# Two chained attention blocks on one core: the f, g, h projections as one block product of 20 instead of 22, with f spilled to DRAM and PSUM in fixed banks

## The chip, the core and the metric

The kernel runs on one core of a Trainium2 chip, in float32 throughout. The metric is device time in microseconds (us) of one launch: the median of three runs before the change is 2583.78 us (2582.63 to 2584.57).

## The reference, cut to what matters

`x` is (8, 512, 64, 64). Two layers follow each other, each added to its input:

```python
def layer0(x):                                  # attention with pooled keys and values
    f = conv1x1(x, Wf, bf)                      # 64 channels x 4096 pixels
    g = maxpool2x2(conv1x1(x, Wg, bg))          # 64 channels x 1024
    v = maxpool2x2(conv1x1(x, Wh, bh))          # 256 channels x 1024
    beta = softmax(einsum('bcn,bcm->bnm', f, g), axis=-1)
    o = einsum('bcm,bnm->bcn', v, beta)         # 256 channels x 4096
    return gamma * conv1x1(o, Wv, bv) + x

def layer1(x):                                  # linear attention
    Q, K, V = wq x + bq, wk x + bk, wv x + bv
    Qf, Kf = delu(Q).T, delu(K)                 # delu(z) = 10*relu(z) + exp(10*min(z, 0))
    KV = einsum('bmn,bcn->bmc', Kf, V)
    norm = 1 / einsum('bnd,bd->bn', Qf, sum(Kf) + 1e-10)
    return x + gamma * einsum('bnd,bdc,bn->bcn', Qf, KV, norm)
```

## The kernel before

The 4096 pixels of an image are cut into 8 chunks of 512, so there are 64 chunks in all (`TOTAL`). One call of `step(s)` works on three things at once: the softmax attention and the layer-1 features of chunk `s` (stage B), the f, g and h projections of chunk `a = s + 9` (stage A; `LEAD` is 9), and the layer-1 end of two chunks of the image before (stage C, on odd steps `finish`). So there are 9 leading steps with stage A alone, 55 middle steps (`s` = 0 to 54) in which A and B run together, and the last image's tail. From `s` = 8 on the odd middle steps carry stage C's product as well: 23 of the 55.

**The order is written by hand.** Each piece of work is entered with a number, `at(t, fn)`; a step sorts its pieces by that number and issues them in this order, and every engine runs its own instructions in that order. The numbers are only an order.

**Stage A** (`a_fg`, `a_h`): f and g are one 128-row product over four input blocks, four matmuls of 512 columns (L272). h is a 2x2x2 block product after Winograd's scheme: 7 products of two 256-column matmuls each (L316), from four sums of x that GpSimd forms (L305 to L308, 128x512 each). In units of one 128x128x256 product, f and g cost 8 and h costs 14, that is 22. VectorE takes h out of PSUM (L326 to L340), pools g and h with reductions (L249), and ScalarE copies f twice into SBUF (L290), where nine such tiles are kept until stage B is nine steps on.

**Stage B**: `weigh` makes the scores of the next chunk (L410, products `s`) and their exponentials (L414, ScalarE, tile `E`). VectorE adds the eight blocks up (L448, L450, L453, tile `r`), a product with ones gives the totals (L467, `tot`), VectorE inverts them (L477, `rq`), two DMAs through DRAM spread the row over the partitions (L482, L484, `rb`), and `keep_inverses` (L497) copies it into a PSUM bank, from which `normalize_block` (L511) multiplies E. `look` (L501, L502) records two checks on ScalarE. `attend` is again seven products (L535, `M1` to `M7`, four 256-column matmuls each) with VectorE sums around them (L517 to L526 for the operands `T1` to `T4`, L544 to L568 for the results). `project` (L598, `N1` to `N7`) makes layer 0's output; ScalarE evicts parts of it (L608), GpSimd and VectorE add them to x (L611, L614, L619). `features` (L645, `pk`) gives layer 1's K and Q.

**Stage C**: `gather` (L739, `pg`) adds K times x transposed into `G`; `normalize` (L861, `pd`) makes the divisors; `finish` (L898, `pa`) has eight products, each copied out by ScalarE (L901) and added to the output by a GpSimd DMA (L904). The transposes of x and K go through DMA (L682, L700) with splitting and joining copies on ScalarE (L694, L707) and GpSimd (L686, `kT`).

All PSUM tiles come from one pool of eight banks in rotation (`bank`, tag "m", `bufs=8`): a product waits until whoever read the product eight places before it is done.

Of the kernel before, what the change touches and what calls it, by code (L numbers as in the profile page):

```python
# [8 lines left out]
F32 = mybir.dt.float32  # L37
U16 = mybir.dt.uint16
# [13 lines left out]
def tile_two_attention_blocks(  # L52
# [40 lines left out]
    w_fg = const.tile([P, KT, 2 * D], F32, name="w_fg")  # L93
    nc.scalar.dma_start(out=w_fg[:, :, 0:D], in_=WfT.rearrange("(k p) o -> p k o", p=P))
    nc.scalar.dma_start(out=w_fg[:, :, D : 2 * D], in_=WgT.rearrange("(k p) o -> p k o", p=P))
    w_h = const.tile([P, KT, CV], F32, name="w_h")
    nc.scalar.dma_start(out=w_h, in_=WhT.rearrange("(k p) o -> p k o", p=P))
    b_fg = const.tile([P, 1], F32, name="b_fg")
    nc.scalar.dma_start(out=b_fg[0:D], in_=bf.rearrange("(p o) -> p o", o=1))
    nc.scalar.dma_start(out=b_fg[D : 2 * D], in_=bg.rearrange("(p o) -> p o", o=1))  # L100
    b_h = const.tile([P, VT], F32, name="b_h")
    nc.scalar.dma_start(out=b_h, in_=bh.rearrange("(k p) -> p k", p=P))
# [24 lines left out]
    def winograd_weights(name, a11, a12, a21, a22, shape):  # L127

        t = const.tile([P, 4] + shape, F32, name=name)
        s1, s2, s3, s4 = (t[:, i] for i in range(4))  # L130

        def form():
            nc.vector.tensor_tensor(s1, a21, a22, ALU.add)
            nc.vector.tensor_tensor(s2, s1, a11, ALU.subtract)
            nc.vector.tensor_tensor(s3, a11, a21, ALU.subtract)
            nc.vector.tensor_tensor(s4, a12, s2, ALU.subtract)

        return {1: a11, 2: a12, 3: s4, 4: a22, 5: s1, 6: s2, 7: s3}, form


    w_h7, form_w_h7 = winograd_weights(
        "w_h7",
        *(w_h[:, bass.ts(j, KT // 2), bass.ts(i, P)] for i in range(2) for j in range(2)),
        [KT // 2, P],
    )
    form_w_h7()
# [21 lines left out]
    def prepare_late():  # L168
        nc.vector.tensor_scalar(gb_v0, b_v0, g0, None, ALU.mult)
        nc.vector.tensor_scalar(w_v, w_v, g0, None, ALU.mult)  # L170
        form_w_v7()
        nc.vector.tensor_scalar(b10_kq, b_kq, PARAM, None, ALU.mult)
        nc.vector.tensor_scalar(b_v1, b_v1, g1, None, ALU.mult)
# [6 lines left out]
    def run(ctx, general):  # L180
# [4 lines left out]
        fpool = ctx.enter_context(tc.tile_pool(name="fpool", bufs=9))  # L185
# [7 lines left out]
        psum = ctx.enter_context(tc.tile_pool(name="psum", bufs=8, space=bass.MemoryType.PSUM))  # L193

        def bank(name):
            return psum.tile([P, CH], F32, tag="m", name=name)

        def scratch(name):
            return temp.tile([P, CH], F32, tag="t", name=name)

# [7 lines left out]
        def load_a(a):  # L208
# [13 lines left out]
            else:  # L222
                if a == 1:
                    nc.gpsimd.tensor_copy(x_a[a][0:1, 0, 0:1], w_fg[0:1, 0, 2 * D - 1 : 2 * D])
# [15 lines left out]
        fgs, fs, vps = {}, {}, {}  # L240

        th, hs, es, sums, totals, rq, rtots, te, os_, to = ({} for _ in range(10))
# [23 lines left out]
        def a_fg(a, at, t, t_f, t_g):  # L266
            j = a % NCHUNK

            def product():
                fg = fgs[a] = bank(f"fg_{a}")  # L270
                for k in range(KT):
                    nc.tensor.matmul(  # L272
                        fg, w_fg[:, k, :], x_a[a][:, k, :], start=(k == 0), stop=(k == KT - 1)
                    )

            def out_g():

                gp = work1.tile([P, P], F32, tag="gp", name=f"gp_{a}")
                pool(gp[D : 2 * D, :], fgs[a][D : 2 * D, :])
                nc.vector.tensor_scalar(  # L280
                    image_of(a)["g"][half(j % 2), j // 2, :], gp[D : 2 * D, :], b_fg[D : 2 * D],
                    None, ALU.add,
                )

            def out_f():

                fg = fgs[a]
                f = fs[a] = fpool.tile([P, CH], F32, tag="f", name=f"f_{a}")
                for e in range(2):
                    nc.scalar.activation(f[half(e)], fg[0:D], AF.Identity, bias=b_fg[0:D])  # L290

            at(t, product)
            at(t_f, out_f)
            at(t_g, out_g)

        def a_h(a, at, t_sums, t, t_out_3, t_pool):
            hk = KT // 2

            def sums_of_x():
                b11, b12, b21, b22 = (  # L300
                    x_a[a][:, bass.ts(i, hk), bass.ts(j, HN)] for i in range(2) for j in range(2)
                )
                ta, tb = blocks(f"tha_{a}", "T2"), blocks(f"thb_{a}", "T3")
                t1, t2, t3, t4 = (u[:, bass.ts(i, hk), :] for u in (ta, tb) for i in range(2))
                nc.gpsimd.tensor_tensor(t1, b12, b11, ALU.subtract)  # L305
                nc.gpsimd.tensor_tensor(t2, b22, t1, ALU.subtract)
                nc.gpsimd.tensor_tensor(t3, b22, b12, ALU.subtract)
                nc.gpsimd.tensor_tensor(t4, t2, b21, ALU.subtract)  # L308
                th[a] = {1: b11, 2: b21, 3: b22, 4: t4, 5: t1, 6: t2, 7: t3}

            m = {}

            def product(i):
                m[i] = bank(f"H{i}_{a}")[:, 0:HN]
                for k in range(hk):
                    nc.tensor.matmul(  # L316
                        m[i], w_h7[i][:, k, :], th[a][i][:, k, :], start=(k == 0), stop=(k == hk - 1)
                    )

            def copy_1():  # L320
                u = m["m1"] = scratch(f"h1_{a}")
                nc.scalar.copy(u[:, 0:HN], m[1])

            def out_1():
                h = hs[a] = blocks(f"h_{a}", "T4").rearrange("p (v j) n -> p v (j n)", v=VT)
                nc.vector.tensor_tensor(h[:, 0, 0:HN], m["m1"][:, 0:HN], m[2], ALU.add)  # L326

            def out_2():
                h, u, w = hs[a], m["m1"], scratch(f"h2_{a}")
                u2, u3 = u[:, HN:CH], w[:, 0:HN]  # L330
                nc.vector.tensor_tensor(u2, u[:, 0:HN], m[6], ALU.add)
                nc.vector.tensor_tensor(h[:, 0, HN:CH], u2, m[5], ALU.add)
                nc.vector.tensor_tensor(h[:, 0, HN:CH], h[:, 0, HN:CH], m[3], ALU.add)
                m["u2"], m["u3"] = u2, u3

            def out_3():
                h, u2, u3 = hs[a], m["u2"], m["u3"]
                nc.vector.tensor_tensor(u3, u2, m[7], ALU.add)
                nc.vector.tensor_tensor(h[:, 1, HN:CH], u3, m[5], ALU.add)
                nc.vector.tensor_tensor(h[:, 1, 0:HN], u3, m[4], ALU.subtract)  # L340

            def out_pool():
                vp = vps[a] = work1.tile([P, VT, P], F32, tag="vp", name=f"vp_{a}")
                for v in range(VT):
                    pool(vp[:, v, :], hs[a][:, v, :])
# [925 lines left out]
```

## Time and profile before

| | |
|---|---|
| median of 3 runs | 2583.78 us |
| span of the profiled execution | 2581.3 us |
| TensorE matmul busy | 2553.4 us, 11223 records |
| VectorE busy | 1951.9 us (76%) |
| ScalarE busy | 1587.9 us (62%) |
| GpSimd busy | 777.6 us (30%) |
| an even middle step without stage C's product, first M product to first M product | 37.29 us |
| an odd one with it | 40.94 us |

Every float32 matmul shows as two records. A record of 256 columns is listed with a mean of about 380 ns, though the next one starts 216 ns later: records overlap (the page says that matmuls are pipelined and their ends modelled). What a product costs the engine is therefore read from start to start in the timeline, not from the mean. The last two rows of the table come from the timeline of TensorE around the middle of the run.

### The profile page before, as it was taken

To read this page: it belongs to the slowest core of one execution; us is meant where nothing else is said; L and a number is where in the kernel's file an instruction comes from. 1 tells how busy PE (TensorE), PEld (TensorE's weight loads), DVE (VectorE), ACT (ScalarE), POOL (GpSimd) and SP (SyncE) were. 2 spreads that over 40 slices of the span, in tenths; PEclk is the share of its full clock that TensorE was granted. 3 is DMA by queue.
4 is the path that set the end of the run, shared out by engine and by line. 5 is a ranking of instruction groups with operands and counts; after the bars stand their busy time and mean duration, and the time that the engine had idled before them with its cause. 6 is when DMAs were issued, how large, how long until landed. Compare 5 with 4: busy or idle time off the path is not lost.

```text
span 2581.3 us, 32122 instructions
## 1 busy us (share of the span) xinstructions
PE 2553.4 (99%) x11223; PEld 1766.8 (68%) x11223; DVE 1951.9 (76%) x3012; ACT 1587.9 (62%) x2724; POOL 777.6 (30%) x624
## 2 busy tenths in 40 slices
PE   9999999999999999999999999999999999999997
PEld 7667766766767667667667677676676676766664
DVE  5777878777777777777777777777777777788874
ACT  3366567567566566675675665666756756656662
POOL 5422223322323323323333223323234232221112
PEclk9999999999999999999999999999999999999998
DMA  5154456566556666665666565765657655655658
GB/s 174 53 141 115 117 142 166 126 174 152 138 167 148 151 178 130 165 167 131 170 161 153 147 153 141 192 140 147 160 133 188 164 132 146 154 143 145 159 141 273
DMA packets 495068, 392.26 MB, mean 152 GB/s; under 512 B 348409, under 2 KB 363697, under 8 KB 494897
## 3 DMA queue, kind: packets, MB, share of 16 engines
q1 hardware_dynamic: 477648, 330.60, 46.8%
q0 software_dynamic: 15232, 58.72, 12.4%
q8 instruction: 91, 1.49, 0.2%
q10 hardware_dynamic: 2016, 0.79, 0.1%
q14 instruction: 81, 0.66, 0.1%
HBM read 173.41 MB, written 133.39 MB: 119 GB/s over the span
## 4 chain that ended last, share of the span: by engine, by line
PE 95%; DVE 3%; issue 0%; DMA 0%; ACT 0%; POOL 0%; ACTq 0%; DVEq 0%
PE M L535 30%; PE H L316 15%; PE N L598 14%; PE s L410 9%; PE pk L645 9%; PE fg L272 8%; PE pg L739 5%; PE pa L898 4%; DVE E L511 1%; PE tot L467 1%; PE pa L977 1%; PE pkv L834 1%; DVE xb L614 0%; DMA w_h<-in_L_conv_Wh_dram 0%; PE pd L861 0%
## 5 line engine op out<-in xcount | busy, mean ns | idle before, releaser
L611 POOL TENSOR_TENSOR xb<-xb,n 128x512 f32<-128x512 f32 x192 | 245.2, 1277 | 464.3 <-ACT n L608 443.4
L535 PE MATMUL M<-T,S 128*128 128x256 f32 x1536 | 363.4, 387 | 0.0
L535 PEld LDWEIGHTS M<-T,S 128*128 128x128 f32 x1536 | 282.2, 190 | 94.1 <-ACT E L414 28.2
L707 ACT COPY xT<-u 128x1024 uint16<-128x1024 uint16 x252 | 328.3, 1354 | 1.4
L511 DVE TENSOR_TENSOR E<-E,rtot 128x1024 f32<-128x1024 f32 x256 | 304.6, 1212 | 32.4 <-ACT rtot L497 30.1
L608 ACT ACTIVATE n<-N,gb_v 128x256 f32<-128x256 f32 x384 | 160.9, 470 | 254.4 <-PE N L598 251.3
L694 ACT COPY w<-xb 128x1024 uint16<-128x1024 uint16 x252 | 244.8, 1042 | 83.5 <-DVE xb L614 83.5
L414 ACT ACTIVATE E<-s 128x512 f32<-128x512 f32 x512 | 256.2, 617 | 33.1 <-PE s L410 26.9
L686 POOL COPY kT<-uk 128x512 uint16<-128x512 uint16 x56 | 68.0, 1214 | 610.8 <-DMA uk<-wk 610.8
L598 PE MATMUL N<-to,w_v 128*128 128x256 f32 x1024 | 243.0, 380 | 2.6 <-ACT n L608 2.6
L410 PE MATMUL s<-f,g 64*128 64x512 f32 x1024 | 238.6, 602 | 0.3 <-DVE o L544 0.3
L645 PE MATMUL pk<-xb,w_kqk 128*128 128x512 f32 x512 | 230.5, 593 | 2.6 <-DVE xb L619 2.6
L535 PE MATMUL M<-E,vT 128*128 128x256 f32 x1024 | 231.5, 379 | 0.0
L614 DVE TENSOR_TENSOR xb<-xb,N 128x512 f32<-128x512 f32 x256 | 174.7, 684 | 72.8 <-POOL xb L611 70.4
L305 POOL TENSOR_TENSOR tha<-xa 128x512 f32<-128x512 f32 x59 | 78.5, 1331 | 482.1 <-PE M L535 445.0
L598 PEld LDWEIGHTS N<-to,w_v 128*128 128x128 f32 x1024 | 193.3, 190 | 31.4 <-ACT n L608 4.2
L535 PEld LDWEIGHTS M<-E,vT 128*128 128x128 f32 x1024 | 194.5, 190 | 26.9 <-issue 0.5
L272 PE MATMUL fg<-xa,w_fg 128*128 128x512 f32 x472 | 212.3, 592 | 0.0
L448 DVE TENSOR_TENSOR r<-E 128x1024 f32<-128x1024 f32 x64 | 78.4, 1225 | 162.7 <-ACT E L414 162.7
L598 PE MATMUL N<-o,w_v 128*128 128x256 f32 x768 | 188.3, 381 | 1.5 <-ACT n L608 0.9
L598 PEld LDWEIGHTS N<-o,w_v 128*128 128x128 f32 x768 | 144.7, 190 | 56.0 <-issue 34.5
L497 ACT COPY rtot<-rb 128x512 f32<-128x512 f32 x54 | 31.8, 590 | 230.1 <-DMA rb<-rd 230.1
(168 smaller groups left out, 4522.2 us busy)
## 6 DMA issues: line engine op xcount, KB each, us to landing
xb<-in_x_dram SPq DMA_DIRECT2D x64, 1024.0 KB
out_dram<-xb SPq DMA_DIRECT2D x63, 1024.0 KB
xa<-in_x_dram SPq DMA_DIRECT2D x59, 1024.0 KB
out_dram<-y POOLq DMA_DIRECT2D x56, 1024.0 KB, 10.5
rb<-rd SPq DMA_DIRECT2D x54, 256.0 KB
w_v<-in_L_conv_wv_dram SPq DMA_DIRECT2D x8, 1024.0 KB
rn<-rn_row SPq DMA_DIRECT2D x56, 128.0 KB
x_early<-in_x_dram SPq DMA_DIRECT2D x4, 1024.0 KB
```

The costliest lines, as they stand in the source:

```text
L272: nc.tensor.matmul(fg, w_fg[:, k, :], x_a[a][:, k, :], start=(k == 0), stop=(k == KT - 1))
L316: nc.tensor.matmul(m[i], w_h7[i][:, k, :], th[a][i][:, k, :], start=(k == 0), stop=(k == hk - 1))
L410: nc.tensor.matmul(sc[e], g[half(e), i, :], fs[s][half(e), :], start=True, stop=True)
L414: nc.scalar.activation(es[s][:, 2 * i + e, :], sc[e], AF.Exp)
L511: nc.vector.tensor_tensor(b, b, r, ALU.mult)
L535: nc.tensor.matmul(m[i], v7[i][:, k, :], te[s][i][:, k, :], start=(k == 0), stop=(k == hm - 1))
L598: nc.tensor.matmul(a[:, k, :], w_v7[i][:, bass.ts(k, P)], b, start=not more and k == 0, stop=True, skip_group_check=more or k > 0,)
L611: nc.gpsimd.tensor_tensor(of_x(*ij), of_x(*ij), u, ALU.add)
L614: nc.vector.tensor_tensor(of_x(*ij), of_x(*ij), m[i], op)
L645: nc.tensor.matmul(pk, w_kqk[:, i, e * D : (e + 2) * D], x_b[s][:, i, :], start=(i == 0), stop=(i == KT - 1),)
L694: nc.scalar.copy(w, x_b[s][:, k, :].bitcast(U16).rearrange("p (n h) -> p h n", h=2))
L707: nc.scalar.copy(v[:, k], u)
```

## The change

It replaces stage A and moves many pieces of work within a step.

- f, g and h become one product of a 3x4 block matrix of weights and a 4x2 block matrix of x (columns: even and odd pixel rows) with 20 block products, each one 256-column matmul (two records). Its weights (`w_p`, 20 blocks) are formed once, at the start. Its operands are single blocks of x or one of 12 sums, formed by 14 additions of 128x256: all on GpSimd, but for the first four on VectorE in the leading steps.
- The 20 products are added up in five chains, A to E, in four fixed PSUM banks (m4 to m7; D follows E in m7). A chain goes on while its partial sums are read: a reader takes the sum as it stands between two products, and the next product of the chain waits for that reader.
- f goes to DRAM (`store_f`) and comes back two steps ahead of its use (`load_f`).
- PSUM: four banks rotate in the middle steps (m0 to m3); the first four of the scores and of `pa` use m4 to m7.
- `keep_inverses` is gone: `normalize_block` multiplies by the row in SBUF (`rb`).
- ScalarE copies `M3` out at once; VectorE copies one of the eight `pa` products.
- New order: M6, M5, M7, M4 before `pg`, then `pg`, `tot`, `pd` in a row; the four `join_x` copies after the exponentials and the `pa` copies; `look` after the inversion and ahead of stage A's first evictions; `features` behind all 20 products. The scaling of Wv moves from VectorE to GpSimd.

The new order of a middle step on TensorE is: M1, M2, M3, eight `s`, (eight `pa`), M6, M5, M7, M4, `pg`, `tot`, (`pd`), products 1 3 8 14 17 2 4, N1, N2, N4, products 5 7 11, N6, N7, products 6 10, N5, products 13 20 9, N3, products 12 16 19 15 18, `pk`. On VectorE it is, from the exponentials on: three additions to `r`, (the copy of a `pa`), M6's sum, the last addition to `r`, the sums of M5, M7, M4 with the operands of `project`, the inversion, (the second inversion), G's addition, three sums of h, a block of E, a sum of f and g, N2's addition, a sum of h, a block of E, N7's addition, two sums of h, and so on.

```diff
-            psum = ctx.enter_context(tc.tile_pool(name="psum", bufs=8, space=bass.MemoryType.PSUM))
-        def bank(name):
-            return psum.tile([P, CH], F32, tag="m", name=name)
+        ring = {"next": 0, "wide": 0}
+        def bank(name, tag=None):
+            if tag is None:
+                tag = f"m{ring['next'] % ring['size']}"
+                ring["next"] += 1
+            return psum.tile([P, CH], F32, tag=tag, name=name)
+        def wide(name, i):
+            return bank(name, None if i > 3 or ring["size"] == 8 else f"m{4 + i}")
...
+        B_SUMS = (
+            ("v18", "b00", "b31", ALU.subtract), ("v14", "b00", "b01", ALU.add),
+            ("v8", "b01", "b21", ALU.subtract), ("v11", "b00", "v8", ALU.add),
+            ("v20", "b01", "b31", ALU.add), ("v20", "b11", "v20", ALU.subtract),
...
+        CHAIN = {
+            1: "A", 2: "A", 5: "A", 6: "A", 9: "A", 15: "A", 18: "A",
+            3: "B", 4: "B", 7: "B", 10: "B", 12: "B",
+            8: "C", 13: "C", 20: "C",
+            14: "E", 17: "E",
+            11: "D", 16: "D", 19: "D",
+        }
+        HEADS = {1: 4, 3: 5, 8: 6, 14: 7, 11: 7}
...
+            def sums(first, last):
+                for i, (to_, x, y, op) in enumerate(B_SUMS[first:last]):
+                    e = nc.vector if s_early and first == 0 else nc.gpsimd
+                    e.tensor_tensor(operand(to_), operand(x), operand(y), op)
+            def product(p):
+                c = CHAIN[p]
+                if p in HEADS:
+                    tag = HEADS[p] - 4 * (s_early and a % 2)
+                    chains[c] = bank(f"{c}_{a}", f"m{tag}")[:, 0:HN]
+                nc.tensor.matmul(
+                    rows_of(chains[c]), w_p[:, p - 1, :], operand(OPERAND[p]), start=p in HEADS,
+                    stop=True, skip_group_check=True,
+                )
+            def into(to_, c, op):
+                nc.vector.tensor_tensor(to_, to_, chains[c], op)
+            def first_20():
...
+                nc.scalar.activation(h(2, 0), chains["A"], AF.Identity, bias=b_h[:, 1:2])
...
+            at(8.2, sums, 0, 4)
+            at(8.21, sums, 4, 14)
...
+            at(t_first[1], first_20)
...
+            at(24.7, lambda: into(acc["fg"], "A", ALU.add))
+            at(27.41, lambda: into(h(1, 1), "A", ALU.subtract))
...
-        def keep_inverses(s):
-            u, rtots[s] = rtots[s], bank(f"rtot_{s}")
-            nc.scalar.copy(rtots[s], u)
...
+                if i == 3:
+                    os_[s] = work1.tile([P, VT, CH], F32, tag="o", name=f"o_{s}")
+                    nc.scalar.copy(os_[s][:, 0, HN:CH], m[3])
...
+            def copy():
+                nc.vector.tensor_copy(m["y"][:, 0, 0, :], m["pa"])
...
+            if ks[0] == 2 and t < 9.0:
+                at(11.85, copy)
...
-                    1: (0.0, None), 2: (1.7, 3.5), 3: (3.9, None), 6: (14.4, 16.1), 5: (16.2, 20.5),
+                    1: (0.0, None), 2: (1.7, 4.0), 3: (3.45, None), 6: (8.8, 11.9), 5: (10.5, 14.0),
+                    7: (12.2, 14.3), 4: (13.9, 15.9),
...
-                    gather(s - 1, at, *((30.9, 32.6) if late_k else (12.6, 13.5)))
+                    gather(s - 1, at, *((30.9, 32.6) if late_k else (15.8, 17.6) if a <= TOTAL else (12.6, 13.5)))
...
-                    t, t_invert = 16.1 if j % 2 == 1 and c_here else 17.85, 18.0
+                    t, t_invert = 16.0, 17.5
...
-                    at(23.0, keep_inverses, n)
...
+                    at(17.55 if 17.4 < t_invert < 18 and a < TOTAL else 26.0 if t_invert > 22 else 21.5, look, n)
```

The order of GpSimd's work changes with it. Before, in a step: the join of `kT`, two pairs of sums of x (each pair after some of the M products), on odd steps two output DMAs, three additions to x. After: the join of `kT`, on odd steps one output DMA (which waits for four `pa` copies), then all 14 sums of x, the first addition to x, on odd steps the other output DMA, two more additions.

## The prediction

> **What bounds the kernel now.** First the page's shares and slices, then the waits of TensorE, then a step's timeline.
>
> ```profile
> PE 2553.4 (99%) x11223; PEld 1766.8 (68%) x11223; DVE 1951.9 (76%) x3012; ACT 1587.9 (62%) x2724; POOL 777.6 (30%) x624
> ...
> PE 95%; DVE 3%; issue 0%; DMA 0%; ACT 0%; POOL 0%; ACTq 0%; DVEq 0%
> ```
>
> TensorE is busy 99% of the span and makes 95% of the chain that ended last. Its own list of waits is nearly empty:
>
> ```profile
> PE N L598 <- ACT n L608: 3.5, 5, 0.9
> PE pk L645 <- DVE xb L619: 2.6, 3, 1.2
> PE row L1226 <- DVE xb L982: 1.7, 1, 1.7
> ```
>
> A dozen entries, 13.5 us in all. So every product removed is gained in full, and every new wait of TensorE is lost in full. The timeline gives the price of a product:
>
> ```profile
> 1269.11 1.89 PE L535 MATMUL M<-E,S 128*128 128x256 f32 x8
> 1270.93 3.70 PE L410 MATMUL s<-f,g 64*128 64x512 f32 x16
> 1274.56 1.94 PE L739 MATMUL pg<-xT,kT 128*64 128x512 f32 x8
> ...
> 1283.99 3.60 PE L272 MATMUL fg<-xa,w_fg 128*128 128x512 f32 x8
> 1287.43 1.89 PE L598 MATMUL N<-o,w_v 128*128 128x256 f32 x8
> ```
>
> From start to start: `fg` 3.44 us for 8 records of 512 columns. Sixteen M records of 256 columns (1265.66 to 1269.11) take 3.45, so 0.216 each.
>
> **The work of TensorE.** Removed per chunk: 3.44 + 28 records of h x 0.216 = 9.49. Added: 40 x 0.216 = 8.64. The saving is 0.85 per chunk, 54 us over 64. `pg` moves beside `tot`, but the number of passages between whole-array products and narrower ones stays (s and pg in one visit, tot in another; now s in one, pg and tot in the other). The stretches around them run 0.1 to 0.2 over their ideal length, as before: 0. Without a new wait the span would be 2581 - 54 = 2527.
>
> **Wait 1: a ring of four banks.** M6 now follows the scores and takes, four places on, the bank of the fifth score. In the even step that begins at 1265.66 the eight exponentials start at 1272.17 and last 3.94: the fifth is read about 2.9 after the first begins, at 9.0 us into the step; TensorE is there at 8.8. Cost 0.25 (between 0.1 and 0.4). In an odd step with `pa`, M6 takes the bank of the fifth `pa`, which VectorE copies behind its three additions to `r`. In the step at 1224.71 these end at 1237.13, 12.4 into the step; the nearest row for the copy is G's (L746, 690 ns): 13.1, where TensorE is at 12.35. Cost 0.7 (0.5 to 0.9). Queued behind M6 is everything.
>
> **Wait 2: VectorE and GpSimd on one port.** This is the term that decides. VectorE and GpSimd late in the same step:
>
> ```profile
> 1282.51 1.34 POOL L307 TENSOR_TENSOR thb<-xa 128x512 f32<-128x512 f32 x1 [1.04 <-PE M L535]
> 1283.82 1.26 POOL L308 TENSOR_TENSOR thb<-tha,xa 128x512 f32<-128x512 f32 x1
> ...
> 1283.09 0.42 DVE L561 TENSOR_TENSOR o<-u,M 128x256 f32<-128x256 f32 x1
> ...
> 1284.53 0.83 DVE L566 TENSOR_TENSOR to<-o,to 128x256 f32<-128x256 f32 x1
> 1285.29 0.41 DVE L567 TENSOR_TENSOR to<-o 128x256 f32<-128x256 f32 x1
> ```
>
> L561, with one operand in PSUM, keeps its 0.42 under GpSimd's addition. L566, with both operands in SBUF, takes 0.83 and ends 0.28 after GpSimd does; L567, the same shape just after, takes 0.41. At the start it is plainer: three 256-column weight sums took 1.00, 1.48 and 1.48 beside GpSimd's additions, the fourth 0.43. The Trainium skill ("SBUF — State Buffer", section "Who interferes with whom") says why: an instruction of VectorE with two SBUF inputs and one of GpSimd that reads SBUF exclude each other, the loser blocking for the whole of the other's instruction. It speaks against this change twice: GpSimd's sums go from 4 to 14 instructions and move under the additions to `r`, and E's scaling loses its PSUM operand. By the rule's worst case an encounter costs a whole GpSimd instruction. By the row it costs what is left of it: 0.41 of a 1.26-long one for L566, about 0.3 on its mean (734 against 429 ns).
>
> Length of a 128x256 sum on GpSimd: not in the trace; half of 1271 ns (L308) is 0.64 and a line from 0.32 (the 128x64 addition at the start) to 1.27 gives 0.73. I take 0.7, so 14 sums take 9.8, plus what VectorE holds them up. In even steps they start after `kT`, about 8 into the step, and run to 18 or later. Between the exponentials and the inversion VectorE has nine instructions with two SBUF operands (three additions to `r`, the last one, the sum M3 + m1, four operands of `project`). Lost per encounter 0.35, half a sum: about 3. VectorE's slack there is 0.5 before M4's result and 0.6 before `tot`, so the inversion comes 1.9 late (0 if no encounter, 5 by the rule's worst case).
>
> Who waits for the inversion? On ScalarE `look` stands right behind it (two checks, 0.8 by the starts 1281.57, 1281.97), and behind `look` stands `first_20`, which must read chain A before product 2. From `tot`'s start: 0.36 + 0.13 to VectorE, 0.98 inversion, 0.80 `look`, 0.47 `first_20` (L608's row), 0.15 hops: 2.9. TensorE reaches product 2 after tot 0.36 and five products x 0.43: 2.5. Late by 0.4 even without the port, by up to 2.3 with it. For even steps I take 1.3, since some sums fall into gaps (ends 0.4 and 3.5). In odd steps with `pa`, GpSimd's output DMA waits for four `pa` copies (12.5) and takes 1.2, so the sums begin near 13.7, behind the additions to `r`; six encounters remain, 2.1 less 1.1 of slack and 0.3 from `pd`: 0.7 (0 to 1.5).
>
> **Wait 3: product 9.** It needs a sum of h (`at(27.41)`) which stands on VectorE behind N7's addition to x, which waits for GpSimd's addition. From N6's end: 0.2 + 0.84 ScalarE, 1.28 GpSimd, 0.69 + 0.42 VectorE, 0.1: 3.5; TensorE does N7, N5 and four products meanwhile: 3.45. Nearly even; but a scaling of E with two SBUF operands (1.2 us, L511) runs just before, and GpSimd's addition must wait for its end. Up to 1.1; I take 0.8 (0.1 to 1.2).
>
> **What is hidden.** VectorE per step: out go 0.70 + 0.33 + 7 x 0.416 + 2 x 0.68 = 5.3; in come 11 sums x 0.42, 0.48, 0.29, 0.69, 0.43 and half a copy: 6.9. So 30.5 (1951.9 / 64) becomes 32, with some 4 of port waits 36 of 39: covered, barely; if uncovered, each us is a us. ScalarE loses 3.2 (copies of f 2 x 0.68, bias 2 x 0.48, 0.37, `rb` 0.59) and gains about as much: 0. f's DMA, 0.4 MB a step against 6 MB: 0. `xT`'s four copies now follow the exponentials: done 16.2 into an even step, where `pg` stands at 15.9: up to 0.3, inside the ends of wait 1. SP's queue: f's loads wait for the scores to be read, ahead of the inversion's DMA, but that reading is over by then: 0.
>
> **Leading steps.** Before, real products began at 6.75 and 5 us of them were done when w_h's sums came (13.62). Now the first needs ten weight sums and four of x on VectorE beside GpSimd from 9.3 on: about 15 to 18. Loss 8. The nine steps then save 0.85 each if TensorE bounds them and lose up to 1.5 if VectorE does (8.4 of 8.6 us, and seven encounters). I take +6 for all (-5 to +20). The tail keeps its order: 0.
>
> **The sum.** Without stage C's product: -0.85 + 0.25 + 1.3 + 0.8 = +1.5, times 32 = 48. With it: -0.85 + 0.7 + 0.7 + 0.8 = +1.35, times 23 = 31. With +6: +85. The profiled execution, 2581.3, becomes 2666; the median stands 2.5 above it: **2669**.
>
> **Rivals.**
> 1. *Faster: the port hardly costs.* VectorE idles 24%, and 2.5 to 3 us a step before `r`. If the sums of x fall mostly into ScalarE's and TensorE's turns, wait 2 is 0.2 and wait 3 is 0.1, and a step costs -0.85 + 0.45 + 0.3 = -0.1 to, with M6 hidden too, -0.7: 2545 to 2578, say 2560. Against: the slack lies before `r`, the sums after its start. It decides if product 2 waits under 0.4. Chance 0.2.
> 2. *No difference:* saving and waits cancel, 2584. Chance 0.05.
> 3. *VectorE becomes the bound:* encounters cost nearly a whole sum (0.6 x 15 = 9 on 32): 41 a step against 39.1, 55 x 2.2 = +120 and the lead +15: 2719 or above. For: 36 of 39 already. Against: mean loss 0.3 in L566's row. Chance 0.15.
> 4. *The 20 products don't run at 0.216* since their x operand skips every second row: no row shows such a read; 10% would be 0.86 a step, and comes under 3.
>
> My forecast has 0.6, with its own range 2615 to 2715. The range for 8 in 10 is 2578 to 2732. A run tells 0.2% (5 us) from no change: faster 0.2, same 0.05, slower 0.75.
>
> **What would show it.** TensorE's list of waits shows product 2 (on ScalarE) and M6 and product 9 (on VectorE) with about 55 entries each; additions to `r` longer than 1.23 in even steps and not in odd ones; a step of 38.8 and 42.3 from M1 to M1. Wrong, if TensorE's share stays at 98% or above, or if additions to `r` keep 1.23.

## The result and the profile after

| | before | after |
|---|---|---|
| median | 2584.18 us (4 runs) | 2720.89 us (2719.72 to 2724.85, 4 runs) |
| span of the profiled execution | 2581.3 us | 2717.8 us |
| ratio, 95% interval | | 1.0534 [1.0519, 1.0549] |

The change makes the kernel 5.3% slower: 136.7 us on the medians, 136.5 on the spans. The forecast was 2669, so the direction and the range for 8 in 10 (2578 to 2732) held. The loss is 1.6 times the 85 us of the sum, and the time lies 6 us above the range that the forecast had kept for its own account (2615 to 2715), where only the third rival (2719 or above) had put it. First the page of the kernel after, its line of busy times:

```profile
PE 2563.6 (94%) x11471; PEld 1816.8 (67%) x11471; DVE 2199.3 (81%) x3339; ACT 1597.3 (59%) x2847; POOL 1205.9 (44%) x1229
```

TensorE falls from 99% to 94%, while no other engine comes near 100%: no engine has taken its place as the bound, TensorE waits. (The record count is no use for the saved products: a pair shows as two records of 256 columns where f and g had records of 512.) What it waits for, in its own list (waiting instruction, engine and instruction waited for, us in total, times, longest):

```profile
PE A L358 <- DVE h L368: 46.0, 56, 6.1
PE M L637 <- DVE y L1020: 22.5, 23, 1.3
PE A L358 <- ACT h L373: 18.5, 44, 0.8
PE s L516 <- DVE o L649: 8.8, 6, 1.5
PE B L358 <- DVE v L351: 6.0, 1, 6.0
```

Before, the whole list came to 13.5 us. The first three lines are the three waits of the forecast: product 9 (waits for a sum of h), M6 (for the copied `pa`), product 2 (for `first_20` on ScalarE). M6's short waits in even steps are not listed. The fourth and the fifth line were not in the forecast: scores at six places, and the very first product. Times at which M1 begins (from TensorE's timeline) cut the span into pieces, and say how much each group of steps lost:

| piece of the run | before | after | sum of the loss |
|---|---|---|---|
| up to the first product of M | 100.15 | 126.25 | +26.1 |
| step 0 | 38.01 | 42.37 | +4.4 |
| steps 1 to 7, mean | 37.29 | 38.33 | +7.3 |
| first step of an image (6), mean | 37.51 | 44.06 | +39.3 |
| second step of an image (6), mean | 42.82 | 44.68 | +11.1 |
| other even steps (18), mean | 37.29 | 38.34 | +18.9 |
| other odd steps (17), mean | 40.88 | 42.47 | +27.0 |
| steps 55 to 62, and the end | | | +2.5 |

### The profile page after: what moved, and what is told of

Read it like the earlier page. It is cut to its first block, busy times and chain, and to the rows that moved or that the text cites. A ratio compares the mean times of both kernels' runs of the same rounds, so it can differ in the third digit from the quotient of the medians.

```text
span 2717.8 us, 34765 instructions
## 1 busy us (share of the span) xinstructions
PE 2563.6 (94%) x11471; PEld 1816.8 (67%) x11471; DVE 2199.3 (81%) x3339; ACT 1597.3 (59%) x2847; POOL 1205.9 (44%) x1229
## 5 line engine op out<-in xcount | busy, mean ns | idle before, releaser
L716 POOL TENSOR_TENSOR xb<-xb,n 128x512 f32<-128x512 f32 x192 | 282.8, 1473 | 409.4 <-ACT n L713 409.4
L794 POOL COPY kT<-wk 128x512 uint16<-128x512 uint16 x56 | 66.5, 1188 | 873.1 <-DMA wk<-wk 873.1
L637 PEld LDWEIGHTS M<-T,S 128*128 128x128 f32 x1536 | 293.1, 194 | 120.3 <-DVE y L1020 41.5
L802 ACT COPY w<-xb 128x1024 uint16<-128x1024 uint16 x252 | 255.3, 1043 | 175.9 <-DVE xb L719 175.9
L613 DVE TENSOR_TENSOR E<-E,rb 128x1024 f32<-128x1024 f32 x220 | 304.4, 1384 | 64.8 <-DMA rb<-rd 64.1
L351 POOL TENSOR_TENSOR v<-xa,v 128x256 f32<-128x256 f32 x410 | 324.9, 804 | 18.3
L351 POOL TENSOR_TENSOR v<-xa 128x256 f32<-128x256 f32 x345 | 324.5, 1013 | 14.5 <-PE A L358 12.8
L358 PE MATMUL A<-v,w_p 128*128 128x256 f32 x640 | 201.0, 398 | 73.4 <-DVE h L368 46.0
L358 PEld LDWEIGHTS A<-v,w_p 128*128 128x128 f32 x640 | 112.2, 190 | 129.6 <-issue 60.1
L556 DVE TENSOR_TENSOR r<-r,E 128x1024 f32<-128x1024 f32 x128 | 172.3, 1346 | 15.1 <-ACT E L520 2.6
```

The costliest lines, as they stand in the source:

```text
L351: e.tensor_tensor(operand(to_), operand(x), operand(y), op)
L358: nc.tensor.matmul(rows_of(chains[c]), w_p[:, p - 1, :], operand(OPERAND[p]), start=p in HEADS, stop=True, skip_group_check=True,)
L613: nc.vector.tensor_tensor(b, b, r, ALU.mult)
L637: nc.tensor.matmul(m[i], v7[i][:, k, :], te[s][i][:, k, :], start=(k == 0), stop=(k == hm - 1))
L716: nc.gpsimd.tensor_tensor(of_x(*ij), of_x(*ij), u, ALU.add)
L802: nc.scalar.copy(w, x_b[s][:, k, :].bitcast(U16).rearrange("p (n h) -> p h n", h=2))
```

## The experiments

All times are medians; the kernel after is 2720.9, and each ratio is to the kernel before (2583 beside each of them). In a kernel whose edit adds three lines, line numbers behind it are higher by 3.

**Product 9's place in VectorE's order.**

```
-            at(27.41, lambda: into(h(1, 1), "A", ALU.subtract))
+            at(27.05 if a >= LEAD else 27.41, lambda: into(h(1, 1), "A", ALU.subtract))
```

> The sum of h before product 9 is moved ahead of N7's addition to x on VectorE, nothing else. My theory (wait 3 is that place in VectorE's order, behind GpSimd's addition): product 9's wait of 0.7 to 0.85 falls below 0.15, 55 steps x 0.7 = 38: about 2683. Rival A (VectorE is late anyway, by the scaling of E just before): half of the wait stays, about 2700. Rival B (the chain of products only hands the wait on to product 12 or to N5): no change, 2715 to 2722.

Measured: 2679.75 us, ratio 1.0368 [1.0351, 1.0385], 41.1 less. This is the list of TensorE's waits in that kernel:

```profile
PE M L637 <- DVE y L1020: 20.8, 23, 1.2
PE A L358 <- ACT h L373: 15.2, 31, 0.8
...
PE A L358 <- DVE h L368: 6.1, 3, 5.3
```

The line that stood first, 46.0 us in 56 waits, is down to 6.1 us in 3, and most of that is the start. The other two lines stay. So the wait was one place in an order. Nearly nothing was handed on: from `pk` to the next M1 it is now 3.54 us instead of 3.43, since VectorE does the addition to x that `pk` needs behind that sum now.

**`look` behind the first evictions.**

```
-    at(17.55 if 17.4 < t_invert < 18 and a < TOTAL else 26.0 if t_invert > 22 else 21.5, look, n)
+    at(18.45 if 17.4 < t_invert < 18 and a < TOTAL else 26.0 if t_invert > 22 else 21.5, look, n)
```

> The two checks of look move on ScalarE from before first_20 to right behind the four first evictions; nothing else. My theory (inversion late by the port, then 0.80 us of checks before first_20): the wait of product 2 goes, 0.5 in even and 0.3 in odd steps: 22 us, 2697 to 2702. Rival A (product 2 waits for the inversion itself or for the evictions, not the checks): within 5 of 2721. Rival B (the wait goes on to product 5 or to a bank): gain under 8 us.

Measured: 2694.8 us, ratio 1.0432 [1.0414, 1.0449], 26.1 less; even steps 38.34 become 37.77, odd ones 42.47 become 42.05. The list of waits of that kernel, its first lines:

```profile
PE A L358 <- DVE h L368: 48.1, 55, 6.1
PE M L637 <- DVE y L1020: 21.5, 23, 1.3
PE s L516 <- DVE o L649: 8.8, 6, 1.5
```

Product 2's line is gone, and the gain (26) is more than that line had held (18.5): the list counts less than a wait costs.

**GpSimd without its sums of x.**

```
                     e = nc.vector if s_early and first == 0 else nc.gpsimd
-                    e.tensor_tensor(operand(to_), operand(x), operand(y), op)
+                    if s_early:
+                        e.tensor_tensor(operand(to_), operand(x), operand(y), op)
+                    else:
+                        e.memset(operand(to_), 0.25)
```

> Leaves out the 14 sums of x that GpSimd forms per chunk in the steps from the last leading one on (each becomes a fill of the same slot with a constant, so GpSimd reads no SBUF there), and scales the scores by 0.001 within the exponentials so that they stay finite; the order and all other instructions stay. Changed kernel: 2721. My theory (VectorE and GpSimd on one port): additions to r fall from 1.35 to 1.23 us on the mean, product 2's wait of 0.4 to 0.6 in even steps goes below 0.2, even steps 38.3 become 37.6 to 37.8, odd ones 42.5 become 42.1 to 42.3: 2685 to 2700. Rival A (look alone stands before first_20, port or not): product 2 still waits 0.4, 2710 to 2720. Rival B (the banks and the new order cost the time): steps as they were, within 5 of 2721. Product 9's wait of 0.7 should stay by every theory, since its partner is GpSimd's addition to x.

Measured: 2693.5 us, ratio 1.0427 [1.0409, 1.0444], 27.4 less, even steps 37.78, odd ones 42.09. Two stretches of VectorE's and GpSimd's timelines (start, us, instruction) show why. The kernel after, an odd step whose M1 begins at 1388.86, VectorE first and one of GpSimd's sums below it:

```profile
1404.61 0.85 DVE L559 TENSOR_TENSOR r<-r 128x512 f32<-128x512 f32 x1
1405.38 0.94 DVE L658 TENSOR_TENSOR o<-o,m 128x256 f32<-128x256 f32 x1
...
1410.42 0.95 DVE L672 TENSOR_TENSOR to<-o 128x256 f32<-128x256 f32 x1
1411.29 0.94 DVE L673 TENSOR_TENSOR to<-to,o 128x256 f32<-128x256 f32 x1
1412.16 0.94 DVE L583 RECIPROCAL rq<-tot 128x128 f32<-128x128 f32 x1
...
1404.98 1.06 POOL L351 TENSOR_TENSOR v<-xa,v 128x256 f32<-128x256 f32 x1
```

The same step where GpSimd only fills (M1 at 1372.66), VectorE first, GpSimd below it, and last two earlier rows:

```profile
1388.41 0.69 DVE L562 TENSOR_TENSOR r<-r 128x512 f32<-128x512 f32 x1
1389.02 0.42 DVE L661 TENSOR_TENSOR o<-o,m 128x256 f32<-128x256 f32 x1
...
1393.93 0.42 DVE L675 TENSOR_TENSOR to<-o 128x256 f32<-128x256 f32 x1
1394.26 0.42 DVE L676 TENSOR_TENSOR to<-to,o 128x256 f32<-128x256 f32 x1
1395.51 0.96 DVE L586 RECIPROCAL rq<-tot 128x128 f32<-128x128 f32 x1 [0.83 <-PE tot L576]
...
1386.12 4.18 POOL L354 MEMSET v<- 128x256 f32 x14
...
1382.52 2.87 DVE L559 TENSOR_TENSOR r<-r,E 128x1024 f32<-128x1024 f32 x2
...
1383.23 1.14 POOL L797 COPY kT<-wk 128x512 uint16<-128x512 uint16 x1 [16.85 <-DMA wk<-wk]
```

A sum of two SBUF tiles takes 0.94 beside GpSimd's sums and 0.42 without them. The inversion begins 23.3 us into the step with the sums and 22.85 without them, and there it has waited 0.83 for `tot`: VectorE has become early. The fills, which write SBUF and read none, hold nothing up (0.42 for L661 in the middle of them). This is the exclusion of two reads that the forecast took from the Trainium skill ("SBUF — State Buffer", "Who interferes with whom"), which also says that a GpSimd instruction that only writes does not take part; these rows agree. What the theory had wrong is where it bites: the additions to `r` lost little to the sums (1346 ns on the mean, 1310 without them; before 1229). They meet GpSimd's copy `kT`, which is there either way: in the last two rows it runs alone beside them, and they take 2.87 for two, as in the kernel after. It is the sums of 256 columns behind them that double.

**The copy of `pa` between the additions to `r`.**

```
-                at(11.85, copy)
+                at(11.0, copy)
```

> VectorE's copy of the fifth pa moves from behind the three additions to r to before the last of them (time 11.0 in place of 11.85), nothing else. My theory (wait 1: M6 takes that bank, so it waits for the copy's place in VectorE's order): the copy ends 1.4 us earlier, M6's wait of 1.04 in the 23 steps with pa falls below 0.2, 23 x 0.9 = 20: about 2701. Rival A (the last addition to r, now 0.7 later, delays M6's result and the sum for tot): the gain comes back as a wait of tot or product 2, under 8. Rival B (four banks are too few, so M6 then waits for another bank): under 8.

Measured: 2703.8 us, ratio 1.0468 [1.0450, 1.0485], 17.1 less. TensorE's timeline in an odd step of the kernel after (the bracket is the wait just before):

```profile
1316.95 3.60 PE L1011 MATMUL pa<-qq,kv 64*128 64x512 f32 x16
1321.53 5.45 PE L637 MATMUL M<-T,S 128*128 128x256 f32 x24 [0.97 <-DVE y L1020]
```

And with the copy moved:

```profile
1387.46 3.60 PE L1011 MATMUL pa<-qq,kv 64*128 64x512 f32 x16
1390.99 5.45 PE L637 MATMUL M<-T,S 128*128 128x256 f32 x24
```

M6 follows the first `pa` after 3.53 us instead of 4.58. Four banks are enough; what counted was when the one reader got to its bank. Odd steps go from 42.47 to 41.72, so 0.3 of the 1.05 comes back further on in the step.

**The sums of v at the start of an image.** `sums_of_v` makes S1 to S4, the operands of M3, M5, M6 and M7, once an image on GpSimd, four additions of 128x512, at the end of the step before. The change left it alone. The first of two experiments takes it out:

```
-            nc.gpsimd.tensor_tensor(s1, a21, a22, ALU.add)
-            nc.gpsimd.tensor_tensor(s2, s1, a11, ALU.subtract)
...
+            nc.gpsimd.memset(s1, 0.25)
+            nc.gpsimd.memset(s2, 0.25)
...
```

> Leaves out the four sums S1 to S4 of v of each image (they become fills with a constant; GpSimd reads no SBUF there). Theory (at an image's start GpSimd's four 512-wide sums hold VectorE's pooling of h and scaling of E, which now read SBUF twice, and the scores wait): pooling instructions back to 0.69 and 0.42 us, scaling to 1.22, the first steps of images fall from 43 to 44 us to 37.5 to 38.5, six times 5 to 6 us: 2685 to 2692, and the granted clock there stays above 0.95. Rival (the first step of an image is long since M3 now stands 0.45 us earlier and waits for S4 itself, or since the image's first step changed in order): the fills are shorter than the sums, so M3 finds them too, but VectorE's instructions are no shorter; under 10 us gained if the cause is the order.

Measured: 2685.5 us, ratio 1.0391 [1.0374, 1.0409], 35.4 less. First steps of images take 38.49 in place of 44.06; other even ones stay (38.35). The timelines of GpSimd, VectorE and TensorE around such a start in the kernel after, that of the fourth image (M1 at 1099.44):

```profile
1097.36 2.02 POOL L498 TENSOR_TENSOR S<-vT 128x512 f32<-128x512 f32 x1 [4.20 <-ACT vT L479]
...
1098.17 1.76 DVE L413 TENSOR_TENSOR hm<-h 128x512 f32<-128x512 f32 x1
1099.96 1.38 DVE L415 TENSOR_TENSOR vp<-hm 128x256 f32<-128x256 f32 x1
1101.27 2.29 DVE L613 TENSOR_TENSOR E<-E,rb 128x1024 f32<-128x1024 f32 x1
1103.59 2.18 DVE L619 TENSOR_TENSOR T<-E 128x1024 f32<-128x1024 f32 x1
...
1107.90 1.12 PE L516 MATMUL s<-f,g 64*128 64x512 f32 x2 [0.35 <-ACT m L642]
1110.49 2.08 PE L516 MATMUL s<-f,g 64*128 64x512 f32 x4 [1.47 <-DVE o L649]
```

And with S left out, the same start (M1 at 1090.46):

```profile
1089.19 0.69 DVE L413 TENSOR_TENSOR hm<-h 128x512 f32<-128x512 f32 x1
1089.91 0.42 DVE L415 TENSOR_TENSOR vp<-hm 128x256 f32<-128x256 f32 x1
1090.27 1.21 DVE L613 TENSOR_TENSOR E<-E,rb 128x1024 f32<-128x1024 f32 x1
1091.51 1.23 DVE L619 TENSOR_TENSOR T<-E 128x1024 f32<-128x1024 f32 x1
```

Four instructions of VectorE take 7.6 us instead of 3.6. Before the change three of them had no second SBUF operand: h was pooled by reductions with one operand, and E's scaling read the inverses from PSUM. At the same start of the kernel before, the sums of v stretched two of the sums for `T` (1.92 and 2.21 us, elsewhere 1.22), and the first step took 37.51, hardly more than the 37.29 of other even ones. A read of the diff for new encounters should have found S, an old instruction with new neighbours. TensorE does five scores without a gap; the sixth waits 0.35 for a bank that ScalarE reads (`m`), the seventh 1.47 for one that VectorE frees too late (`o`), and then the clock falls. Windows of the same stretch of the kernel after (us, PE, PEld, DVE, ACT and POOL busy with counts, granted clock of TensorE, share of DMA, GB/s):

```profile
1104.70:1107.90 3.20, 2.85 (x11) 1.06 (x10) 3.20 (x5) 1.47 (x3) 0.00 (x0) 1.00 1.06 337
1107.90:1110.40 2.50, 1.12 (x2) 0.29 (x2) 2.31 (x10) 2.20 (x5) 0.25 (x1) 0.87 0.62 124
1110.40:1112.60 2.20, 2.08 (x4) 0.51 (x4) 2.20 (x3) 0.58 (x2) 2.20 (x3) 0.50 0.86 203
1112.60:1116.00 3.40, 3.33 (x8) 2.70 (x9) 3.19 (x3) 3.38 (x6) 3.32 (x3) 0.50 1.04 398
1116.00:1119.90 3.90, 3.90 (x19) 3.37 (x18) 3.76 (x6) 3.59 (x4) 3.82 (x4) 0.92 0.52 158
```

In narrower windows the clock is at half from 1109.77 to 1116.59: 24 records of M take 7.2 us (1112.67 to 1119.88) where they take 5.2 (24 x 0.216). With S left out the two stretches that answer to these, 8 to 20 us into the step, have a clock of 1.00. The start of the third image (M1 at 768.60) has the same waits of 0.35 and 1.47, but its clock stays at 1.00, and M runs at its usual pace:

```profile
779.65 1.13 PE L516 MATMUL s<-f,g 64*128 64x512 f32 x4 [1.47 <-DVE o L649]
781.47 5.45 PE L637 MATMUL M<-T,S 128*128 128x256 f32 x24 [0.69 <-ACT E L520]
```

That step takes 42.85 us. The five first steps with a fall take 43.70 to 44.68. So of the 6.55 that a first step loses on the mean (44.06 - 37.51), 5.3 come without any fall of the clock, and the clock makes 1.2 (44.06 - 42.85). The second experiment keeps the sums and splits them:

```
-                    at(29.25 if early else 39.0, sums_of_v, (a - 1) // NCHUNK)
+                    if early:
+                        at(29.25, sums_of_v, 0)
+                    else:
+                        at(28.3, sums_of_v, (a - 1) // NCHUNK, 0, 3)
+                        at(39.0, sums_of_v, (a - 1) // NCHUNK, 3, 4)
```

> The sums S1 to S4 of v are formed in two parts: three of the four slots in the last step of the image before (time 28.3, after GpSimd's three additions to x), the last slot where all of it stood. Theory (GpSimd's four 512-wide sums at the start of an image hold VectorE): the part left there takes some 1.5 to 2 us in place of 7, and the first steps of images lose 3.5 to 5 of the 5 to 6 us that leaving S out brought; the last steps before gain up to 1: 2690 to 2704. Rival (the encounters only move to the end of the step before, with VectorE's chain to the next E): under 10.

Measured: 2700.1 us, ratio 1.0454 [1.0436, 1.0471], 20.8 less. The first steps of images take 39.89, so 25.0 came back there; 4.8 of it went in step 55, where the last image's part collides with an order of its own (41.02 where it had been 36.23).

**The start.** All sums of x of the first two chunks on VectorE:

```
-                    e = nc.vector if s_early and first == 0 else nc.gpsimd
+                    e = nc.vector if s_early and (first == 0 or a < 2) else nc.gpsimd
```

> The 14 sums of x of the first two chunks all go to VectorE, so GpSimd reads no SBUF while VectorE forms the 25 sums of the weights; nothing else. Theory (the start is late since VectorE's sums of the weights meet GpSimd's sums of x: 0.29 us alone, 0.81 beside): the sums of the weights take 0.29 each, the first product moves from 14.3 to 13, product 5 of chunk 0 from 25.3 to 21 to 22.5; the first product of M from 126 to 120 to 124, 2715 to 2719. Rival (the start is bound by the number of sums, wherever they stand): VectorE has 20 sums x 0.34 = 6.8 us more, product 5 comes at 26 or later and the total is 2721 to 2728.

Measured: 2713.6 us, ratio 1.0508 [1.0491, 1.0526], 7.3 less. VectorE's timeline at the start of the kernel after, with one of GpSimd's sums beside it:

```profile
9.15 0.81 POOL L351 TENSOR_TENSOR v<-x_early,v 128x256 f32<-128x256 f32 x1
9.29 0.81 DVE L112 TENSOR_TENSOR spare<-w_h 128x128 f32<-128x128 f32 x1
10.03 0.81 DVE L115 TENSOR_TENSOR w_p<-w_p,spare 128x128 f32<-128x128 f32 x1
```

and in the experiment:

```profile
8.89 0.28 DVE L112 TENSOR_TENSOR spare<-w_h 128x128 f32<-128x128 f32 x1
9.09 0.28 DVE L115 TENSOR_TENSOR w_p<-w_p,spare 128x128 f32<-128x128 f32 x1
```

The first product moves from 14.29 to 11.35, product 5 of the first chunk from 25.25 to 21.18, the first product of M from 126.25 to 120.45. VectorE does 20 more instructions and is done earlier. But 20 of the 26 us stay.

**Four edits together**: product 9, `look`, the copy of `pa`, S in two parts.

> Four edits together: product 9's sum first, look behind the evictions, the copy of pa between the additions to r, S in two parts. If the waits are separate, as my theory has it, the gains add up: 41 + 26 + 20 + 24 = 111: 2600 to 2620. Rival (they are one lateness of VectorE that each edit shifts, so that together they bring little more than the largest): 2650 or above. No theory has it below 2585, since the 26 us of the start stay.

Measured: 2622.8 us, ratio 1.0151 [1.0134, 1.0168]: 98.1 less, where the four alone brought 41.1 + 26.1 + 17.1 + 20.8 = 105.1. It lies 3 us above the range expected. The waits are separate. Of the missing 7 us the start has 3.4: the first product of M comes at 129.69, where kernels with the same start had it between 124.7 and 128.4, a spread that no edit here explains.

**The four edits, and no sums of x.**

> The four edits, and beside them the 14 sums of x per chunk from the last leading step on replaced by fills (left out; scores scaled by 0.001 within the exponentials so that they stay finite). It asks what is left of the even steps, 37.0 to 37.3 where the sum had 36.44. If VectorE's lateness by GpSimd's sums still costs there: even steps 36.5 to 36.8, the total 2590 to 2605. If the rest is the passages between products and the remaining hops, which the sums of x have no part in: even steps stay at 37.0 to 37.2, the total 2612 to 2622.

Measured: 2604.6 us, ratio 1.0085 [1.0069, 1.0100], 18.2 less than with the sums. The even steps go from 37.30 to 36.74, most of them to 36.70, where the sum had 36.44. So with the three waits out of the way GpSimd's sums still cost an even step 0.56, and 0.26 is left. Two rows of such a step (M1 at 895.27; line numbers are higher by 6 here), loads of weights on TensorE, say where:

```profile
904.31 5.05 PEld L643 LDWEIGHTS M<-T,S 128*128 128x128 f32 x24 [0.89 <-ACT E L526]
...
928.43 0.30 PEld L758 LDWEIGHTS pk<-xb,w_kqk 128*128 128x128 f32 x2 [0.25 <-DVE xb L730]
```

M6 waits for the fifth exponential: it starts 3.77 us after the first score, where the product behind the scores started 3.63 after it before. That is wait 1 of the forecast, at 0.14. `pk` waits for VectorE's last addition to x, and M1 comes 3.53 after it instead of 3.43. The two make 0.24. The new passages between products, which the forecast had put at 0, are 0 on balance: M6, M5, M7, M4 and product 1 take 7.64 us for 34 records of 0.216 (7.34), 0.30 over; before, M6, M5 and M7 took 5.48 for 24 (5.18), 0.30 over too.

**The kernel before without its PSUM operand.**

```
-                    at(23.0, keep_inverses, n)
+                    at(23.0, lambda: bank(f"unused_{n}"))
```

> The kernel before, with keep_inverses left away: E's scaling reads the inverses from SBUF, as in the changed kernel, and not from the bank that ScalarE copied them to (a bank is still passed over, so the others keep their places). Before: 2583. My theory (with two SBUF operands the scaling takes part in the exclusion with GpSimd): its instructions rise from 1.21 us to 1.28 to 1.45 on the mean, GpSimd's additions to x from 1.28 to 1.35 or more; TensorE has most of that covered, so the time rises only by 2 to 25: 2585 to 2608. Rival (the second operand's place does not matter): 1.21 stays, and the time is 2583 or up to 5 less, since ScalarE has a copy less and the scaling starts earlier.

Measured: 2583.3 us, ratio 1.0000 [0.9992, 1.0008]. Groups of instructions of the kernel before (busy us, mean ns | idle time ahead of them):

```profile
L511 DVE TENSOR_TENSOR E<-E,rtot 128x1024 f32<-128x1024 f32 x256 | 304.6, 1212 | 32.4 <-ACT rtot L497 30.1 <-PE rtot L491 1.2 <-ACT tot L502 0.2
L611 POOL TENSOR_TENSOR xb<-xb,n 128x512 f32<-128x512 f32 x192 | 245.2, 1277 | 464.3 <-ACT n L608 443.4 <-DMA rn<-rn_row 20.9
```

and with the inverses read from SBUF:

```profile
L511 DVE TENSOR_TENSOR E<-E,rb 128x1024 f32<-128x1024 f32 x216 | 335.5, 1574 | 14.5 <-DMA rb<-rd 13.7
L611 POOL TENSOR_TENSOR xb<-xb,n 128x512 f32<-128x512 f32 x192 | 286.6, 1493 | 423.9 <-ACT n L608 402.9 <-DMA rn<-rn_row 20.9
```

The scaling grows by 0.36 us each (0.07 to 0.24 had been expected), 74 us of VectorE's time in all (335.5 - 216 x 1.212), GpSimd's additions by 0.22 each, and the program takes exactly as long. Both theories fell in part: the operand's place does make the encounters, and they cost nothing here, where TensorE, busy 99% of the span, waits for neither chain.

**With the start and two more places.** On top of the four edits: the start's sums on VectorE as above, and the first four of the ninth chunk's; the pooling of the leading chunks behind the next sum of f and g; three additions to `r` earlier in the last leading step; the last image's S in one part; and in the middle steps

```
-            at(t + 3.8, add, (0, 0), 2, ALU.add)
+            at(t + (3.8 if last else 3.82), add, (0, 0), 2, ALU.add)
...
-    ts.get(n, (36.6, 24.0, 32.3, 25.2) if a < TOTAL else (24.3, 26.0, 27.3, 29.2))
+    ts.get(n, (36.6, 24.0, 32.3, 27.06) if a < TOTAL else (24.3, 26.0, 27.3, 29.2))
```

> The four edits (S of the last image in one part again, which should give back the 4.5 us of the step at 55), with the start: sums of x of the first two chunks and the first four of the ninth on VectorE, the pooling of h of the leading chunks behind fg's sum, the first additions to r ahead of the sums of h in the step before the first; and two more places in the order of VectorE (N2's addition to x behind the sum of h, the second scaling of E behind product 9's sum). Expected from the traces: start -9 to -16, step 55 -4.5, even steps -0.1 to -0.2: 2595 to 2608. It should still not beat 2583, since the first leading products wait for 25 sums of weights. Rival (the start has another bound behind these, such as the granted clock or ScalarE's first evictions): 2612 or above.

Measured: 2607.4 us, ratio 1.0093 [1.0078, 1.0109]. Even steps take 37.05, other odd ones 40.58, both now under the kernel before (37.29 and 40.88); step 55 is back at 36.23. The start is at 119.33, hardly better than VectorE's sums alone (120.45): with the additions to `r` earlier, product 5 of the ninth chunk waits 2.3 us for a sum of h instead. Against before the start still costs 19.2, step 0 4.3 and the first steps of images 7.3; the other even and odd steps behind `s` = 8 give 9.4 back. No version tried beats the kernel before.

## Why the prediction was right, and where it was not

**The saving** (-0.85 per chunk): the products run at their price. In the timelines a product takes 0.43 us from start to start, the two records of 0.216 that the sum had used, so rival 4, a slow read of every second row, is out. An even step without the sums of x and the three places in the order took 36.70, which is 37.29 - 0.85 + 0.14 (M6) + 0.10 (`pk`) to within 0.02. So this term was right, and so was nothing for the passages.

**Wait 1**: right in kind. In an even step M6 stood 0.14 late (3.77 for 3.63; 0.25 forecast, with a slip in its working: by the row, the fifth exponential ends 2.5 us after the first begins, not 2.9, which its own "9.0 us into the step" agrees with), in an odd one 1.05 (4.58 for 3.53; 0.7 forecast; the copy comes behind additions to `r` that `kT` had lengthened). Moving the copy gave 0.74 for each of the 23 steps.

**Wait 2** ("the term that decides"): right in kind, too large in size. The inversion was late by GpSimd's sums, and product 2 waited for it behind `look`. By the two experiments that was 0.57 in an even and 0.4 in an odd step, where the sum had 1.3 and 0.7. Taking away either of the two parts, the sums of x or `look`'s place, gives the same 26 to 27 us. What was to show it did not: the additions to `r` were longer in odd steps too, by `kT`. The encounters lay later, in the last addition to `r` (876 ns on the mean, 717 without the sums) and in the operands of `project`.

**Wait 3**: right. Moving the one sum gave 41 us, 0.75 in each of 55 steps for a forecast of 0.8. It was the largest of the three.

**The middle step's sum** came out close by luck: wait 2 was too large, odd M6 too small, and the two kinds of step missed in opposite directions. Even steps took 38.34 (38.8 forecast) and odd ones 42.47 (42.3). All of the middle steps but the six that start an image lost 68.7 us (4.4 + 7.3 + 11.1 + 18.9 + 27.0); the same 49 steps at the forecast's 1.5 and 1.35 would be 70. But the 26 without stage C's product lost 1.18 each, and the 23 with it 1.66.

**The step that failed is the count of the middle steps, "times 32 = 48" and "times 23 = 31".** It knew 55 steps of two kinds. The six that start an image lost 39.3, where it had given them 6 x 1.5 = 9: a miss of 30 us. It had looked for encounters with the new instructions on GpSimd only; S is an old one, which met new two-operand instructions of VectorE. Taking S out gave 33.4 of these 39.3 back, some 7 of it by the clock (six times 1.2).

**The leading steps** ("I take +6 for all (-5 to +20)") cost 26, the other term that failed. That the first product comes at "about 15 to 18" was nearly right (14.29). But only seven products can run on that first half; product 5 needed the second half and the sum of h behind it, and waited 6.1 us until 25.25. TensorE had by then done 3.0 us of work where before it had done some 17. The clock added to it: eight products took 6.5 us (25.25 to 31.71) for the usual 3.5.

That is not all: behind product 5 a leading chunk takes 9.7 us where it took 9.5 before, though it has 0.85 less of products. TensorE waits there 4.9 us in six places for a sum of f and g on VectorE, once 3.9 for GpSimd's sums of the ninth chunk, and once 3.2 at `tot` for the additions to `r`. The forecast had named that ("lose up to 1.5 if VectorE does"), but 26 lies above its whole range. Of the loss, the experiment on the start gave back 6. The other 20 are read from the timeline as the number and the order of the sums, with the clock; no run separates these, and none took the weights' sums away.

**Rivals.** The port costs, so the first is out; product 2 waited 0.42 on the mean of its 44 entries, just over the 0.4 from which that rival would have decided. The second is out by the ratio. The third had the time right (2719 or above) and its mechanism wrong: it had 41 us for every middle step by VectorE as the bound, where most even ones took 38.34 and VectorE was busy 81%; only at the starts of images was it busy almost without a pause (3.20 of 3.20 us, 2.31 of 2.50 and 2.20 of 2.20 in the windows above). The time lies in the range for 8 in 10 only because that range reached into this rival's. The +85 of the sum became +136.5 by 20 of the lead and 30 of the six steps.

## What to carry to other kernels

When a change gives an instruction a second SBUF operand, look for every GpSimd instruction that may run beside it, old ones and rare ones too, and step through one of each kind of step, not only the common one. A longer instruction costs nothing by itself (74 us on VectorE cost nothing in the kernel before): ask what the first instruction of the bounding engine is that stands behind it, and by how much it was early. When several such waits appear, the cheap cure is the order: three moved lines, each tried alone, gave back 41, 26 and 17 of 137 us here without a single instruction less.

## What the runs showed of the hardware that was not expected

- At the starts of images the granted clock fell without a long gap, and everywhere it fell in fixed portions. At the start of the fourth image TensorE had waited 0.35 us and was 0.75 into a wait of 1.47 when its clock went to 0.50. In windows of 0.02 us the kernel after has nine stretches at half clock before its end: they begin at 10.67, 24.33, 119.90, 447.58, 1109.77, 1444.27, 1771.95, 2106.46 and 2440.96 us, last 6.83 or 3.41, and all their ends and beginnings lie whole multiples of 3.413 us apart (within 0.01). Five of the six first steps of images have one, of either length, and the third image's has none with the same waits. What within a portion decides is not shown.
- GpSimd's uint16 copy `kT`, with no sum of x beside it, lengthened the additions to `r` (2.87 us for two, where two took 2.55 in the kernel before), while fills lengthened no two-operand sum of VectorE (0.42 us).
- The list of waits holds less than waits cost: product 2's line had 18.5 us, and removing it brought 26.1.
